# One-pass layer norm with the scale moved to the mask and to adj, and squares summed before the norm product, in a two-layer graph kernel

## The chip, the cores and the metric

The kernel runs on one core of a Trainium2 chip. The metric is the device time of one execution in microseconds (us). The runs of one kernel agreed within 0.12%; the mean granted TensorE clock of the timed runs was 0.996 to 0.999. TensorE is called PE in the profile (PEld is its weight load), VectorE is DVE, ScalarE is ACT, GpSimd is POOL. L128 is line 128 of the kernel; the numbers differ between kernels, so the tile names (pg, pv, pn ...) are the better guide. PSUM is the memory into which the matmuls of this kernel write, and a record is one instruction as the profile lists it.

## The reference, cut to what matters

x is (64, 256, 512) fp32, adj is (256, 256) of zeros and ones with 3% ones.

```python
# layer 0
h = jnp.maximum(_layernorm(x), 0.0)
q, k, v = h @ Wq.T, h @ Wk.T, h @ Wv.T          # per batch element, written as einsums
rel = adj.T[None] * (q @ k^T)
rel = rel / jnp.linalg.norm(rel, axis=2, keepdims=True)
x = x + rel @ v
# layer 1
h = jnp.maximum(_layernorm(x), 0.0)
x = x + (adj @ h) @ weight + bias
```

## The kernel before

It works on 32 pairs of batch elements (512 tokens in four chunks of 128). All matmuls are fp32. `pt` are TensorE transposes of h, `pg` and `pv` the two projections of layer 0, `prel` the scores, `pu` the product with v, `pn` the row norms, `py` and `po` the two products of layer 1. The parts that the change and the argument touch:

```python
def norm_relu(dst, src):                      # both layers; tiles st, mv, rs left out
    for c in range(TC):
        nc.vector.bn_stats(st[:, c, :], src[:, c, :])
        nc.vector.bn_aggr(mv[:, c, :], st[:, c, :])
    nc.vector.tensor_scalar(rs, mv[:, :, 1], 0.0, EPS, op0=ALU.max, op1=ALU.add)
    nc.scalar.activation(rs, rs, AF.Sqrt)
    nc.vector.reciprocal(rs, rs)
    for c in range(TC):
        nc.vector.tensor_scalar(dst[:, c, :], src[:, c, :], mv[:, c, 0:1], rs[:, c : c + 1],
                                op0=ALU.subtract, op1=ALU.mult)
        nc.vector.scalar_tensor_tensor(dst[:, c, :], dst[:, c, :], 0.0, dst[:, c, :],
                                       op0=ALU.is_gt, op1=ALU.mult)
# ... scores(i): prel matmuls, then for each batch element b
            nc.vector.tensor_mul(rel[:, b], pm, adj_sb)
            nc.scalar.activation(sq[:, b], rel[:, b], AF.Square)
# ... attend(i): pu matmuls, then the norm product
                for m in range(NC):
                    nc.tensor.matmul(pn[:, c : c + 1], sq[:, b, m, ts(n, P)], ones,
                                     start=(m == 0), stop=(m == NC - 1))
# ... ln1(i): norm_relu, then the bias is added to the residual on GpSimd
            nc.gpsimd.tensor_tensor(X[i][:, c, :], X[i][:, c, :], bias_bc, ALU.add)
# ... the loop over pairs
    for i in range(NP):
        # ... load(i + 3)
        scores(i)
        if nxt:
            transposes(i + 1)
        attend(i)
        ln1(i)
        if nxt:
            project_g(i + 1); project_v(i + 1)
        # ... ln0(i + 2)
        gather_mix(i)                         # py, po, output
```

Of the kernel before, what the change touches and what calls it, by code (L numbers as in the profile page):

```python
# [9 lines left out]
F32 = mybir.dt.float32  # L10
AF = mybir.ActivationFunctionType
ALU = mybir.AluOpType
EPS = 1e-5
# [3 lines left out]
def kernel(  # L17
# [8 lines left out]
    bias: bass.AP,  # L26
    out: bass.AP,
):
    """Two pre-norm graph layers, worked on two batch elements (512 tokens) at a time.

    Layer 0 uses q k^T = h (Wq^T Wk) h^T with Wq^T Wk formed once, keeps the masked
    scores transposed ([m, n], so that adj is read as it lies and the scores are the
    stationary operand of the product with v), and divides by the row norms after that
    product.  Layer 1 forms (adj h)^T directly, so it needs no transposes of h.
    The residual stream of a pair stays in one SBUF tile from its load to its store.
    """
    nc = tc.nc
    P = 128
    B, N, D = x.shape
    DC = D // P  # L40
    NC = N // P
    NB = 2
    TC = NB * NC
    T = NB * N
# [7 lines left out]
    work = ctx.enter_context(tc.tile_pool(name="work", bufs=2))  # L52
    small = ctx.enter_context(tc.tile_pool(name="small", bufs=3))
# [1 line left out]
    ps_m = ctx.enter_context(tc.tile_pool(name="ps_m", bufs=5, space=bass.MemoryType.PSUM))  # L55
    ps_n = ctx.enter_context(tc.tile_pool(name="ps_n", bufs=1, space=bass.MemoryType.PSUM))

    X, H, HT, G, V, R, H2 = {}, {}, {}, {}, {}, {}, {}

    def load(i):  # L60
        X[i] = xpool.tile([P, TC, D], F32, tag="x", name=f"x_{i}")
        nc.sync.dma_start(out=X[i], in_=xs[i])

# [1 line left out]
    load(0)  # L65
    ident = const.tile([P, P], F32, name="ident")
    make_identity(nc, ident)
    ones = const.tile([P, 1], F32, name="ones")
# [8 lines left out]
    adj_sb = const.tile([P, NC, N], F32, name="adj_sb")  # L77
# [5 lines left out]
        out=bias_bc, in_=bass.AP(tensor=bias.tensor, offset=bias.offset, ap=[[0, P], [1, D]])  # L83
    )

    def norm_relu(dst, src):
        """dst = max(layernorm(src), 0), as (t > 0) * t so that a NaN stays one.

        A row with a NaN has one as its mean; its variance is kept out of the square root.
        """  # L90
        st = small.tile([P, TC, 6], F32, tag="st", name="st")
        mv = small.tile([P, TC, 2], F32, tag="mv", name="mv")
        rs = small.tile([P, TC], F32, tag="rs", name="rs")
        for c in range(TC):
            nc.vector.bn_stats(st[:, c, :], src[:, c, :])  # L95
            nc.vector.bn_aggr(mv[:, c, :], st[:, c, :])
        nc.vector.tensor_scalar(rs, mv[:, :, 1], 0.0, EPS, op0=ALU.max, op1=ALU.add)
        nc.scalar.activation(rs, rs, AF.Sqrt)
        nc.vector.reciprocal(rs, rs)
        for c in range(TC):  # L100
            nc.vector.tensor_scalar(  # L101
                dst[:, c, :], src[:, c, :], mv[:, c, 0:1], rs[:, c : c + 1],
                op0=ALU.subtract, op1=ALU.mult,
            )
            nc.vector.scalar_tensor_tensor(  # L105
                dst[:, c, :], dst[:, c, :], 0.0, dst[:, c, :], op0=ALU.is_gt, op1=ALU.mult
            )

# [1 line left out]
    def ln0(i):  # L110
        H[i] = work.tile([P, TC, D], F32, tag="h", name=f"h_{i}")
        norm_relu(H[i], X[i])

    def transposes(i):
        h = H.pop(i)
# [27 lines left out]
            nc.scalar.copy(V[i][:, c, :], pm[:, :D])  # L143

    def scores(i):
        ht, g = HT.pop(i), G.pop(i)
        rel = work.tile([P, NB, NC, N], F32, tag="rel", name=f"rel_{i}")
        sq = work.tile([P, NB, NC, N], F32, tag="sq", name=f"sq_{i}")
        for b in range(NB):
            pm = ps_m.tile([P, NC, N], F32, tag="pm", name="prel")  # L150
            for m in range(NC):
                for e in range(DC):
                    nc.tensor.matmul(  # L153
                        pm[:, m, :], ht[:, e, ts(b * NC + m, P)], g[:, e, ts(b, N)],
                        start=(e == 0), stop=(e == DC - 1),
                    )
            nc.vector.tensor_mul(rel[:, b], pm, adj_sb)  # L157
            nc.scalar.activation(sq[:, b], rel[:, b], AF.Square)  # L158
        R[i] = (rel, sq)

    def attend(i):
        (rel, sq), v = R.pop(i), V.pop(i)
        pu = []
        for b in range(NB):
            for n in range(NC):
                pm = ps_m.tile([P, 512], F32, tag="pm", name="pu")
                for m in range(NC):
                    nc.tensor.matmul(  # L168
                        pm[:, :D], rel[:, b, m, ts(n, P)], v[:, b * NC + m, :],
                        start=(m == 0), stop=(m == NC - 1),  # L170
                    )
                pu.append(pm)
        pn = ps_n.tile([P, TC], F32, tag="pn", name="pn")
        for b in range(NB):
            for n in range(NC):
                c = b * NC + n
                for m in range(NC):
                    nc.tensor.matmul(  # L178
                        pn[:, c : c + 1], sq[:, b, m, ts(n, P)], ones,
                        start=(m == 0), stop=(m == NC - 1),  # L180
                    )
        rn = small.tile([P, TC], F32, tag="rn", name="rn")
        nc.scalar.activation(rn, pn, AF.Sqrt)  # L183
        nc.vector.reciprocal(rn, rn)  # L184
        for c in range(TC):
            nc.vector.scalar_tensor_tensor(  # L186
                X[i][:, c, :], pu[c][:, :D], rn[:, c : c + 1], X[i][:, c, :],
                op0=ALU.mult, op1=ALU.add,
            )

# [1 line left out]
    def ln1(i):  # L192
        H2[i] = work.tile([P, TC, D], F32, tag="h2", name=f"h2_{i}")
        norm_relu(H2[i], X[i])
        for c in range(TC):
            nc.gpsimd.tensor_tensor(X[i][:, c, :], X[i][:, c, :], bias_bc, ALU.add)  # L196

    def gather_mix(i):
        h2, xt = H2.pop(i), X.pop(i)
        yt = work.tile([P, DC, T], F32, tag="yt", name=f"yt_{i}")  # L200
        for b in range(NB):
            for d0 in range(0, DC, 2):
                pm = ps_m.tile([P, 2, N], F32, tag="pm", name="py")
                for d in range(2):
                    for m in range(NC):
                        nc.tensor.matmul(  # L206
                            pm[:, d, :], h2[:, b * NC + m, ts(d0 + d, P)], adjt_sb[:, m, :],
                            start=(m == 0), stop=(m == NC - 1),
                        )
                nc.scalar.copy(yt[:, d0 : d0 + 2, ts(b, N)], pm)  # L210
        for c in range(TC):
            pm = ps_m.tile([P, 512], F32, tag="pm", name="po")
            for d in range(DC):
                nc.tensor.matmul(  # L214
                    pm[:, :D], yt[:, d, ts(c, P)], w_sb[:, d, :],
                    start=(d == 0), stop=(d == DC - 1),
                )
            nc.vector.tensor_add(xt[:, c, :], pm[:, :D], xt[:, c, :])  # L218
        nc.gpsimd.dma_start(out=outs[i], in_=xt)  # L219

# [1 line left out]
    m_sb = const.tile([P, DC, D], F32, name="m_sb")  # L222
    for d in range(DC):
        pm = ps_m.tile([P, 512], F32, tag="pm", name="pw")
        for e in range(DC):
            nc.tensor.matmul(  # L226
                pm[:, :D], wq_sb[:, e, ts(d, P)], wk_sb[:, e, :],
                start=(e == 0), stop=(e == DC - 1),
# [8 lines left out]
    adjt_sb = const.tile([P, NC, N], F32, name="adjt_sb")  # L237
# [3 lines left out]
            nc.tensor.transpose(pt[:, m * N + n * P : m * N + (n + 1) * P], adj_sb[:, n, ts(m, P)], ident)  # L241
    nc.scalar.copy(adjt_sb, pt[:, : NC * N].rearrange("p (m n) -> p m n", m=NC))

# [1 line left out]
    ln0(0)  # L245
    for j in (1, 2):
        if j < NP:
# [4 lines left out]
    if NP > 1:  # L252
        ln0(1)
    for i in range(NP):
        nxt = i + 1 < NP
        if i + 3 < NP:
            load(i + 3)
# [6 lines that stand above are left out]
            project_g(i + 1)  # L264
            project_v(i + 1)
        if i + 2 < NP:
            ln0(i + 2)
        gather_mix(i)
# [28 lines left out]
```

## Time and profile before

| | before |
|---|---|
| median time | 2161.83 us (2160.5 to 2161.97, 3 runs) |
| TensorE busy | 98% of the span |
| VectorE, ScalarE, GpSimd busy | 38%, 16%, 12% |
| period of one pair on TensorE | 65.64 us |
| TensorE's waits at the start, in the last pair | 19.7 us, 9.9 us |

A period is read from the chain in order of time: the distance between the starts of the same group, here pv, in two pairs that follow each other. It repeats within 0.02 us in all middle pairs of a trace.

### The profile page before, as it was taken

To read this page: it belongs to the slowest core of one execution; us is meant where nothing else is said; L and a number is where in the kernel's file an instruction comes from. 1 tells how busy PE (TensorE), PEld (TensorE's weight loads), DVE (VectorE), ACT (ScalarE), POOL (GpSimd) and SP (SyncE) were. 2 spreads that over 40 slices of the span, in tenths; PEclk is the share of its full clock that TensorE was granted. 3 is DMA by queue.
4 is the path that set the end of the run, shared out by engine and by line. 5 is a ranking of instruction groups with operands and counts; after the bars stand their busy time and mean duration, and the time that the engine had idled before them with its cause. 6 is when DMAs were issued, how large, how long until landed. Compare 5 with 4: busy or idle time off the path is not lost.

```text
span 2159.8 us, 16275 instructions
## 1 busy us (share of the span) xinstructions
PE 2122.4 (98%) x6708; PEld 1190.1 (55%) x6708; DVE 812.5 (38%) x1504; ACT 348.9 (16%) x682; POOL 257.0 (12%) x170
## 2 busy tenths in 40 slices
PE   6999999999999999999999999999999999999996
PEld 3555555555555555555555555555555555555554
DVE  2422444323444324444234443234442244442333
ACT  1111111111111111111111111111111111111110
POOL 0101111101111001111011111011110011110111
PEclk9999999999999999999999999999999999999998
DMA  4011001111011110011110011110111100110001
GB/s 165 0 39 39 12 28 39 39 40 39 1 39 39 39 39 21 19 39 39 39 39 5 35 39 39 39 39 1 39 39 39 39 20 20 39 39 20 20 1 39
DMA packets 27689, 72.86 MB, mean 34 GB/s; under 512 B 1120, under 2 KB 1120, under 8 KB 27616
## 3 DMA queue, kind: packets, MB, share of 16 engines
q1 hardware_dynamic: 16896, 33.56, 4.6%
q0 software_dynamic: 9136, 35.13, 4.3%
q10 hardware_dynamic: 1584, 3.15, 0.4%
q8 instruction: 52, 0.85, 0.2%
q14 instruction: 21, 0.17, 0.0%
HBM read 38.27 MB, written 33.55 MB: 33 GB/s over the span
## 4 chain that ended last, share of the span: by engine, by line
PE 97%; issue 1%; DMA 1%; DVE 1%; POOL 0%; ACT 0%; POOLq 0%; ACTq 0%; DVEq 0%
PE pg L128 21%; PE pv L139 20%; PE po L214 20%; PE prel L153 10%; PE pu L168 10%; PE py L206 10%; PE pt L120 3%; PE pn L178 2%; DMA wk_sb<-in_L_gnn_Wk_dram 1%; PE pw L226 1%; POOL x L196 0%; DVE h L105 0%; DVE x L186 0%; DVE st L95 0%; DVE h L101 0%
## 5 line engine op out<-in xcount | busy, mean ns | idle before, releaser
L128 PE MATMUL pg<-ht,m_sb 128*128 128x512 f32 x1024 | 447.4, 595 | 0.0
L139 PE MATMUL pv<-wvt_sb,ht 128*128 128x512 f32 x1024 | 444.7, 592 | 0.0
L214 PE MATMUL po<-w_sb,yt 128*128 128x512 f32 x1024 | 444.7, 592 | 0.0
L218 DVE TENSOR_TENSOR x<-po,x 128x512 f32<-128x512 f32 x128 | 88.6, 692 | 777.7 <-PE po L214 777.7
L196 POOL TENSOR_TENSOR x<-x,bias_bc 128x512 f32<-128x512 f32 x128 | 229.5, 1821 | 850.3 <-DVE h L101 850.3
L139 PEld LDWEIGHTS pv<-wvt_sb,ht 128*128 128x128 f32 x1024 | 194.6, 190 | 244.9 <-issue 244.9
L214 PEld LDWEIGHTS po<-w_sb,yt 128*128 128x128 f32 x1024 | 194.6, 190 | 231.3 <-issue 229.6
L128 PEld LDWEIGHTS pg<-ht,m_sb 128*128 128x128 f32 x1024 | 192.0, 190 | 229.1 <-issue 228.2
L206 PE MATMUL py<-adjt_sb,h 128*128 128x256 f32 x1024 | 229.0, 382 | 9.9 <-DVE h L105 9.9
L105 DVE SCALAR_TENSOR_TENSOR h<-h 128x512 f32<-128x512 f32 x256 | 233.3, 953 | 0.0
L168 PE MATMUL pu<-v,rel 128*128 128x512 f32 x512 | 230.1, 592 | 0.0
L153 PE MATMUL prel<-g,ht 128*128 128x256 f32 x1024 | 226.2, 379 | 0.0
L206 PEld LDWEIGHTS py<-adjt_sb,h 128*128 128x128 f32 x1024 | 196.0, 192 | 50.7 <-issue 24.4
L153 PEld LDWEIGHTS prel<-g,ht 128*128 128x128 f32 x1024 | 194.6, 190 | 40.1 <-issue 15.3
L101 DVE TENSOR_SCALAR h<-x,mv,rs 128x512 f32<-128x512 f32 x256 | 186.7, 771 | 1.2
L95 DVE BATCH_NORM_STATS2 st<-x 128x6 f32<-128x512 f32 x256 | 167.3, 669 | 15.4 <-DMA x<-in_x_dram 15.4
L219 POOL DMA_DIRECT2D out_dram<-x x32 | 24.6, 770 | 1046.3 <-DVE x L218 1046.3
L168 PEld LDWEIGHTS pu<-v,rel 128*128 128x128 f32 x512 | 92.4, 190 | 92.4 <-issue 92.3
L158 ACT ACTIVATE sq<-rel 128x512 f32<-128x512 f32 x64 | 40.4, 631 | 545.3 <-DVE rel L157 545.3
L184 DVE RECIPROCAL rn<-rn 128x4 f32<-128x4 f32 x32 | 5.7, 178 | 319.0 <-ACT rn L183 319.0
L157 DVE TENSOR_TENSOR rel<-prel,adj_sb 128x512 f32<-128x512 f32 x64 | 44.3, 692 | 214.0 <-PE prel L153 214.0
L132 ACT COPY g<-pg 128x512 f32<-128x512 f32 x128 | 74.4, 581 | 289.0 <-PE pg L128 289.0
(33 smaller groups left out, 680.7 us busy)
## 6 DMA issues: line engine op xcount, KB each, us to landing
x<-in_x_dram SPq DMA_DIRECT2D x32, 1024.0 KB, 5.2
out_dram<-x POOLq DMA_DIRECT2D x32, 1024.0 KB, 4.7
wq_sb<-in_L_gnn_Wq_dram ACTq DMA_DIRECT2D x1, 1024.0 KB, 12.1
wk_sb<-in_L_gnn_Wk_dram ACTq DMA_DIRECT2D x1, 1024.0 KB, 18.4
wv_sb<-in_L_gnn_Wv_dram ACTq DMA_DIRECT2D x1, 1024.0 KB, 23.2
w_sb<-in_L_gnn_weight_dram POOLq DMA_DIRECT2D x1, 1024.0 KB, 11.7
adj_sb<-in_adj_dram POOLq DMA_DIRECT2D x1, 256.0 KB, 7.4
bias_bc<-in_L_gnn_bias_dram POOLq DMA_DIRECT2D x1, 256.0 KB, 12.4
```

Source lines behind the costliest of these rows:

```text
L95: nc.vector.bn_stats(st[:, c, :], src[:, c, :])
L101: nc.vector.tensor_scalar(dst[:, c, :], src[:, c, :], mv[:, c, 0:1], rs[:, c : c + 1], op0=ALU.subtract, op1=ALU.mult,)
L105: nc.vector.scalar_tensor_tensor(dst[:, c, :], dst[:, c, :], 0.0, dst[:, c, :], op0=ALU.is_gt, op1=ALU.mult)
L128: nc.tensor.matmul(pm[:, :T], m_sb[:, d, ts(e, P)], HT[i][:, d, :], start=(d == 0), stop=(d == DC - 1),)
L132: nc.scalar.copy(G[i][:, e, :], pm[:, :T])
L139: nc.tensor.matmul(pm[:, :D], HT[i][:, d, ts(c, P)], wvt_sb[:, d, :], start=(d == 0), stop=(d == DC - 1),)
L153: nc.tensor.matmul(pm[:, m, :], ht[:, e, ts(b * NC + m, P)], g[:, e, ts(b, N)], start=(e == 0), stop=(e == DC - 1),)
L168: nc.tensor.matmul(pm[:, :D], rel[:, b, m, ts(n, P)], v[:, b * NC + m, :], start=(m == 0), stop=(m == NC - 1),)
L196: nc.gpsimd.tensor_tensor(X[i][:, c, :], X[i][:, c, :], bias_bc, ALU.add)
L206: nc.tensor.matmul(pm[:, d, :], h2[:, b * NC + m, ts(d0 + d, P)], adjt_sb[:, m, :], start=(m == 0), stop=(m == NC - 1),)
L214: nc.tensor.matmul(pm[:, :D], yt[:, d, ts(c, P)], w_sb[:, d, :], start=(d == 0), stop=(d == DC - 1),)
L218: nc.vector.tensor_add(xt[:, c, :], pm[:, :D], xt[:, c, :])
```

## The change

The intent is to take work off VectorE and TensorE. A row's relu(layernorm) is relu(x - mean) times 1/std. That factor goes along with the token, so in layer 0 it is put into the mask (1/variance, since the token's factor enters its score and its v) and in layer 1 into a scaled copy of the transposed adj for each batch element. One pass of 128x512 takes the place of two. The squares of the two token chunks are summed on VectorE, so that the norm product needs 4 matmuls a pair in place of 8.

```diff
-        for c in range(TC):
-            nc.vector.tensor_scalar(dst, src, mean, rs, op0=ALU.subtract, op1=ALU.mult)
-            nc.vector.scalar_tensor_tensor(dst, dst, 0.0, dst, op0=ALU.is_gt, op1=ALU.mult)
+        for c in range(TC):     # arguments shortened here
+            nc.vector.tensor_scalar(dst, src, mean, 0.0, op0=ALU.subtract, op1=ALU.max)
 ... layer 0: r2 = 1/var (+ 0 * mean, to keep a NaN), std = sqrt(var)
-            nc.vector.tensor_mul(rel[:, b], pm, adj_sb)
-            nc.scalar.activation(sq[:, b], rel[:, b], AF.Square)
+            for m in range(NC):
+                c = b * NC + m
+                nc.vector.scalar_tensor_tensor(
+                    rel[:, b, m, :], pm[:, m, :], r2[:, c : c + 1], adj_sb[:, m, :],
+                    op0=ALU.mult, op1=ALU.mult,
+                )
+                nc.scalar.activation(
+                    sq[:, b, m, :], rel[:, b, m, :], AF.Square, scale=std[:, c : c + 1]
+                )
+        nc.vector.tensor_add(sqs, sq[:, :, 0, :], sq[:, :, 1, :])
 ...
-                for m in range(NC):
-                    nc.tensor.matmul(
-                        pn[:, c : c + 1], sq[:, b, m, ts(n, P)], ones,
-                        start=(m == 0), stop=(m == NC - 1),
-                    )
+                nc.tensor.matmul(
+                    pn[:, c : c + 1], sqs[:, b, ts(n, P)], ones, start=True, stop=True
+                )
 ... layer 1: rs = 1/sqrt(var) (+ 0 * mean)
+                nc.scalar.activation(
+                    adjb[:, b, m, :], adjt_sb[:, m, :], AF.Copy, scale=rs[:, c : c + 1]
+                )
 ...
-                            pm[:, d, :], h2[:, b * NC + m, ts(d0 + d, P)], adjt_sb[:, m, :],
+                            pm[:, d, :], h2[:, b * NC + m, ts(d0 + d, P)], adjb[:, b, m, :],
```

More of the change, by code (lines that the diff above doesn't have):

```diff
@@ L56 @@
     ps_n = ctx.enter_context(tc.tile_pool(name="ps_n", bufs=1, space=bass.MemoryType.PSUM))
-    X, H, HT, G, V, R, H2 = {}, {}, {}, {}, {}, {}, {}
+    X, H, HT, G, V, R, H2, SC = {}, {}, {}, {}, {}, {}, {}, {}
     def load(i):
@@ L84, with stats @@
     )
-    def norm_relu(dst, src):
+    def stats(src):
         st = small.tile([P, TC, 6], F32, tag="st", name="st")
         mv = small.tile([P, TC, 2], F32, tag="mv", name="mv")
-        rs = small.tile([P, TC], F32, tag="rs", name="rs")
+        ve = small.tile([P, TC], F32, tag="ve", name="ve")
         for c in range(TC):
@@ L96, in norm_relu, with keep_nan, centred_relu @@
             nc.vector.bn_aggr(mv[:, c, :], st[:, c, :])
-        nc.vector.tensor_scalar(rs, mv[:, :, 1], 0.0, EPS, op0=ALU.max, op1=ALU.add)
-        nc.scalar.activation(rs, rs, AF.Sqrt)
-        nc.vector.reciprocal(rs, rs)
+        nc.vector.tensor_scalar(ve, mv[:, :, 1], 0.0, EPS, op0=ALU.max, op1=ALU.add)
+        return mv, ve
+    def keep_nan(dst, mv, src):
+        nc.vector.scalar_tensor_tensor(dst, mv[:, :, 0], 0.0, src, op0=ALU.mult, op1=ALU.add)
+    def centred_relu(dst, src, mv):
         for c in range(TC):
             nc.vector.tensor_scalar(
-                dst[:, c, :], src[:, c, :], mv[:, c, 0:1], rs[:, c : c + 1],
-                op0=ALU.subtract, op1=ALU.mult,
-            )
-            nc.vector.scalar_tensor_tensor(
-                dst[:, c, :], dst[:, c, :], 0.0, dst[:, c, :], op0=ALU.is_gt, op1=ALU.mult
+                dst[:, c, :], src[:, c, :], mv[:, c, 0:1], 0.0, op0=ALU.subtract, op1=ALU.max
             )
@@ L111, in ln0 @@
         H[i] = work.tile([P, TC, D], F32, tag="h", name=f"h_{i}")
-        norm_relu(H[i], X[i])
+        mv, ve = stats(X[i])
+        r2 = small.tile([P, TC], F32, tag="r2", name="r2")
+        std = small.tile([P, TC], F32, tag="std", name="std")
+        nc.vector.reciprocal(r2, ve)
+        keep_nan(r2, mv, r2)
+        nc.scalar.activation(std, ve, AF.Sqrt)
+        centred_relu(H[i], X[i], mv)
+        SC[i] = (r2, std)
     def transposes(i):
@@ L145, in scores @@
     def scores(i):
-        ht, g = HT.pop(i), G.pop(i)
+        ht, g, (r2, std) = HT.pop(i), G.pop(i), SC.pop(i)
         rel = work.tile([P, NB, NC, N], F32, tag="rel", name=f"rel_{i}")
@@ L156, in scores @@
                     )
-            nc.vector.tensor_mul(rel[:, b], pm, adj_sb)
-            nc.scalar.activation(sq[:, b], rel[:, b], AF.Square)
-        R[i] = (rel, sq)
+            for m in range(NC):
[7 more added lines that the diff above has]
+                )
+        sqs = work.tile([P, NB, N], F32, tag="sqs", name=f"sqs_{i}")
+        nc.vector.tensor_add(sqs, sq[:, :, 0, :], sq[:, :, 1, :])
+        R[i] = (rel, sqs)
     def attend(i):
-        (rel, sq), v = R.pop(i), V.pop(i)
+        (rel, sqs), v = R.pop(i), V.pop(i)
         pu = []
@@ L176, in attend @@
                 c = b * NC + n
-                for m in range(NC):
-                    nc.tensor.matmul(
-                        pn[:, c : c + 1], sq[:, b, m, ts(n, P)], ones,
-                        start=(m == 0), stop=(m == NC - 1),
-                    )
+                nc.tensor.matmul(
+                    pn[:, c : c + 1], sqs[:, b, ts(n, P)], ones, start=True, stop=True
+                )
         rn = small.tile([P, TC], F32, tag="rn", name="rn")
@@ L192, in ln1 @@
     def ln1(i):
-        H2[i] = work.tile([P, TC, D], F32, tag="h2", name=f"h2_{i}")
-        norm_relu(H2[i], X[i])
+        h2 = work.tile([P, TC, D], F32, tag="h2", name=f"h2_{i}")
+        adjb = work.tile([P, NB, NC, N], F32, tag="adjb", name=f"adjb_{i}")
+        mv, ve = stats(X[i])
+        rs = small.tile([P, TC], F32, tag="rs", name="rs")
+        nc.scalar.activation(rs, ve, AF.Sqrt)
+        nc.vector.reciprocal(rs, rs)
+        keep_nan(rs, mv, rs)
+        centred_relu(h2, X[i], mv)
+        for b in range(NB):
+            for m in range(NC):
+                c = b * NC + m
+                nc.scalar.activation(
+                    adjb[:, b, m, :], adjt_sb[:, m, :], AF.Copy, scale=rs[:, c : c + 1]
+                )
+        H2[i] = (h2, adjb)
         for c in range(TC):
@@ L198, in gather_mix @@
     def gather_mix(i):
-        h2, xt = H2.pop(i), X.pop(i)
+        (h2, adjb), xt = H2.pop(i), X.pop(i)
         yt = work.tile([P, DC, T], F32, tag="yt", name=f"yt_{i}")
```

## The prediction

> **What bounds the kernel now.** I read the page's first part, then the chain of waits that ended last, then the costliest groups of TensorE, and last the timeline of one pair of batch elements. The page:
>
> ```profile
> PE 2122.4 (98%) x6708; PEld 1190.1 (55%) x6708; DVE 812.5 (38%) x1504; ACT 348.9 (16%) x682; POOL 257.0 (12%) x170
> ...
> PE 97%; issue 1%; DMA 1%; DVE 1%; POOL 0%; ACT 0%; POOLq 0%; ACTq 0%; DVEq 0%
> PE pg L128 21%; PE pv L139 20%; PE po L214 20%; PE prel L153 10%; PE pu L168 10%; PE py L206 10%; PE pt L120 3%; PE pn L178 2%; DMA wk_sb<-in_L_gnn_Wk_dram 1%; PE pw L226 1%; POOL x L196 0%; DVE h L105 0%; DVE x L186 0%; DVE st L95 0%; DVE h L101 0%
> ```
>
> TensorE is busy 98% of the span, and the chain stays on it for 97%. VectorE's 812.5 us and ScalarE's 348.9 us run beside it. So only two things can shorten the kernel: fewer or shorter matmuls, or less of the little time in which TensorE waits. The waits of TensorE itself are:
>
> ```profile
> PE pw L226 <- DMA wk_sb<-in_L_gnn_Wk_dram: 19.7, 1, 19.7
> PE py L206 <- DVE h L105: 9.9, 2, 9.5
> ```
>
> The first is the load of the weights at the start, which the change leaves alone. The second comes once, in the last pair, where no next pair covers the layer norm of layer 1. All other pairs repeat every 65.64 us: the chain has the pv group start at 1019.25 and again at 1084.89.
>
> The matmul that the change halves, in the groups by shape and in a timeline window of one pair:
>
> ```profile
> L178 PE MATMUL pn<-ones,sq 128*128 128x1 f32 x512 | 58.9, 245 | 0.0
> ```
> ```profile
> 1003.57 1.84 PE L178 MATMUL pn<-ones,sq 128*128 128x1 f32 x16
> ...
> 1005.27 13.98 PE L128 MATMUL pg<-ht,m_sb 128*128 128x512 f32 x32
> ```
>
> The reader is to see that a pair has 16 records (the program has 8, each fp32 matmul leaves two) and that they hold TensorE from 1003.57 to 1005.27, 1.70 us, or 0.106 us a record; the mean of 245 ns is latency, since records overlap.
>
> A second, small loss is in the order of transposes and products, in the same pair one step on:
>
> ```profile
> 1061.24 1.02 PE L168 MATMUL pu<-v,rel 128*128 128x512 f32 x2
> 1061.54 0.63 ACT L158 ACTIVATE sq<-rel 128x512 f32<-128x512 f32 x1
> ...
> 1062.07 1.91 ACT L121 COPY ht<-pt 128x512 f32<-128x512 f32 x3
> 1062.10 1.26 PE L120 MATMUL pt<-ident,h 128*128 128x128 f32 x8
> ...
> 1062.70 0.42 PEld L120 LDWEIGHTS pt<-ident,h 128*128 128x128 f32 x4 [0.24 <-ACT ht L121]
> 1063.09 0.30 PEld L168 LDWEIGHTS pu<-v,rel 128*128 128x128 f32 x2
> 1063.19 1.02 PE L168 MATMUL pu<-v,rel 128*128 128x512 f32 x2
> ```
>
> The last eight transposes hold TensorE for 1.09 us (1062.10 to 1063.19), the first eight 0.87 us (1060.37 to 1061.24). The fourth group of four needs a PSUM buffer that ScalarE's second copy frees; the copy stood behind the square, and TensorE lost 0.22 us.
>
> **What the Trainium skill says.** TensorE: Matmul & The Clock Gate, LDWEIGHTS: a weight load takes about P/1.2 ns, P its columns, so 107 ns for 128. The trace agrees: 106 ns a record, though only one column is streamed. The norm product is bound by its weight loads, so halving their number halves its time. FP8 and Floating Point Precision, TensorE Precision Notes: true fp32 takes four passes. With the 2.4 GHz gap of N/2.4 + 2.5 ns (first page, Back-to-back issue gap) that makes an estimate of 4 x 216 = 863 ns for 512 columns; the trace has 13.73 us for 16 of pv, 858 ns. The big products run at their floor and cannot gain. SBUF — State Buffer, Who interferes with whom: VectorE with two SBUF inputs, or in a two-port mode, blocks against GpSimd. The trace agrees: in the last pair, beside the bias add, two passes of L105 took 3.42 us where two took 1.29 us elsewhere.
>
> **The change part by part.**
> 1. Norm product: 4 program matmuls a pair in place of 8, so 8 records x 0.106 us = 0.85 us, x 32 pairs = **27.2 us**, all of it on the path. The sum of squares that allows it, one 128x512 add on VectorE, is about 0.69 us (the like add L218), 22 us in all, hidden: squares are done near 1062.4, so the sum near 1063.2, and pn starts at 1069.2.
> 2. Layer norm, second pass removed on VectorE (L105, 233.3 us). The first pass stays in form, 517 to 544 ns where nothing interferes. Off the path except in the last pair.
> 3. Mask: two 128x512 multiplies (692 ns) become four 128x256 with a pointer scalar. From L186 (745 ns for 512 elements, of which 512/0.96 = 533 ns stream) I estimate 212 + 267 = 479 ns, 61 us in all for 44. The second half is ready near 1060.57 + 0.96 = 1061.53, where the products that need it begin after 1064: no wait.
> 4. ScalarE: 128 squares of 256 for 64 of 512, and 128 scaled copies of adj^T. Estimated from the square's 631 ns: 631 - 213 (256/1.2) = 418, near 450 ns with a pointer for scale; +18 and +58 us, total some 425 us of 2130. The copies end some 10 us after pn; py starts 27.5 us after it. Hidden.
> 5. Order. The instruction order of the changed kernel has the transposes as 8, pu, 4, pu, 4 instead of 8, pu, 8. A pu lasts 0.86 us, so the fourth group is wanted near 1063.4, and the second copy, behind two short squares, ends near 1063.0. The 0.22 us should go: 31 x 0.22 = 6.8 us at most; I count **5 us**.
> 6. Last pair: from the end of pn (2119.3) to po (2138.82) is 19.5 us, 6.91 of them py's work. New chain after pn: root and reciprocal 0.5, residual 2.73, statistics to the variance 2.77 with two centred passes between them 1.0, then root, reciprocal, two more passes and the NaN step 1.5 to 3.5 (GpSimd's bias add interferes), a scaled copy 0.4: 8.9 to 10.9, plus py 6.9 without stalls. That gains 1.7 to 3.7; I count **2 us**.
>
> The large products keep shape and number. Sum: 2161.8 - 27.2 - 5 - 2 = 2127.6, so 2128 us, 1.6% less.
>
> **Rivals.**
> (a) VectorE's 200 us of saved passes come through. Against it: TensorE waits for VectorE only 9.9 us in all. For a 2% gain the saving must reach 43 us; parts 1, 5 and 6 at their largest give 27.2 + 6.8 + 3.7 = 37.7, so about 2124.
> (b) A new wait replaces the loads: the chain mask, square, sum, pn now crosses to ScalarE and back to VectorE. It has some 6 us of slack by the times in part 1; only a ScalarE blocked behind its in-order queue could use it up. If each pair lost 0.85 us there, the time would stay at 2155.
> (c) ScalarE's root or scaled copies hold back the copies of g, and so PSUM. The copies of g are 3.4 us apart and take 0.6; four scaled copies take some 1.8 us. If each pair lost 0.3 us, 2138.
> (d) The order gain of part 5 does not come, the rest does: 2133.
>
> **Range and chances.** The norm term is almost certain, which puts everything without new waits between 2124 and 2135; half a chance of a small loss as in (c) widens it to 2121 to 2140. Faster by 2% would need 2118.6, below what the terms give: 3%. Slower by 2%: 1%, for a wait that I have not seen. Within 2%: 96%.
>
> **What would show it right or wrong.** pn with 256 records and about 27 us on the chain; a period of about 64.6 us between pairs; VectorE near 620 us and ScalarE near 425; no wait of TensorE for squares, sums or scaled copies except the last pair's; the fourth group of transposes without a wait for ScalarE. A period above 65 us with TensorE idle ahead of pn, pu or pg would make the prediction wrong.

## The result, and the profile after

The changed kernel took 2127.65 us (median of 4 runs, 2127.24 to 2128.48), the kernel before 2161.59 in the same rounds. The ratio is 0.9846, with a 95% interval of 0.9832 to 0.986. A ratio here is taken from the runs of both kernels, and is not quite the ratio of the medians. The result lies within 0.4 us of the predicted 2128 and is 1.5% faster, in the class "within 2%".

The page of the changed kernel, the engines and the chain:

```profile
PE 2086.4 (98%) x6452; PEld 1160.6 (55%) x6452; DVE 642.0 (30%) x1408; ACT 417.3 (20%) x874; POOL 209.2 (10%) x170
...
PE 97%; issue 1%; DMA 1%; DVE 0%; POOL 0%; ACT 0%; POOLq 0%; ACTq 0%; DVEq 0%
PE pg L136 21%; PE pv L147 21%; PE po L247 20%; PE prel L165 10%; PE pu L189 10%; PE py L239 10%; PE pt L128 3%; PE pn L198 1%; DMA wk_sb<-in_L_gnn_Wk_dram 1%; PE pw L259 1%; POOL x L229 0%; DVE x L205 0%; DVE st L94 0%; ACT wvt_sb L269 0%; POOLq L325 0%
```

VectorE gave up 170 us of busy time and ScalarE took on 68, and TensorE is still at 98% and still is the chain. Its busy time fell by 36 us, its records by 256, all of them pn. The waits of TensorE and the group of pn:

```profile
PE pw L259 <- DMA wk_sb<-in_L_gnn_Wk_dram: 19.7, 1, 19.7
...
PE py L239 <- ACT adjb L224: 11.3, 1, 11.3
```
```profile
L198 PE MATMUL pn<-ones,sqs 128*128 128x1 f32 x256 | 30.3, 240 | 0.0
```

The wait at the start is as before. The wait in the last pair did not shrink: it grew from 9.9 to 11.3 us and is now for the scaled copies of adj. One pair in the timeline (first column the start, second the duration):

```profile
1044.26 1.02 PE L189 MATMUL pu<-v,rel 128*128 128x512 f32 x2
...
1045.12 0.60 PE L128 MATMUL pt<-ident,h 128*128 128x128 f32 x4
...
1045.56 1.02 PE L189 MATMUL pu<-v,rel 128*128 128x512 f32 x2
1045.99 0.14 PEld L128 LDWEIGHTS pt<-ident,h 128*128 128x128 f32 x1 [0.24 <-ACT ht L129]
1046.42 0.60 PE L128 MATMUL pt<-ident,h 128*128 128x128 f32 x4
...
1046.85 5.32 PE L189 MATMUL pu<-v,rel 128*128 128x512 f32 x12
...
1052.01 0.95 PE L198 MATMUL pn<-ones,sqs 128*128 128x1 f32 x8
...
1052.82 13.98 PE L136 MATMUL pg<-ht,m_sb 128*128 128x512 f32 x32
```

Two things are to be seen. pn holds TensorE from 1052.01 to 1052.82, 0.81 us where it had held it for 1.70. And a product of 0.86 us now lies between the two last groups of transposes: the weight load still waits for ScalarE's copy (0.24 us), but it does so while that product runs, and the two groups take 0.44 and 0.43 us in place of 1.09 together.

The period is 64.53 us (pv starts at 1002.27 and 1066.79), 1.11 less. The spans of the two profiled runs differ by 2159.8 - 2125.1 = 34.7 us. The first pv starts 0.35 us earlier (55.35 and 55.00), which is within scatter: over the kernels here that load in the same way it starts between 54.34 and 55.56 us; from there to the last pv it is 2014.13 and 1979.70 us, 34.43 less; from the last pv to the end it is 90.32 and 90.40, so the last pair gained nothing although its pn is 0.89 us shorter. That sets the question: two terms in the pairs, and a loss of about 1 us at the end.

### The profile page after: what moved, and what is told of

Same layout as the page of the kernel before. It is cut to its first block, busy times and chain, and to the rows that moved or that the text cites. A ratio compares the mean times of both kernels' runs of the same rounds, so it can differ in the third digit from the quotient of the medians.

```text
span 2125.1 us, 15806 instructions
## 1 busy us (share of the span) xinstructions
PE 2086.4 (98%) x6452; PEld 1160.6 (55%) x6452; DVE 642.0 (30%) x1408; ACT 417.3 (20%) x874; POOL 209.2 (10%) x170
## 4 chain that ended last, share of the span: by engine, by line
PE 97%; issue 1%; DMA 1%; DVE 0%; POOL 0%; ACT 0%; POOLq 0%; ACTq 0%; DVEq 0%
PE pg L136 21%; PE pv L147 21%; PE po L247 20%; PE prel L165 10%; PE pu L189 10%; PE py L239 10%; PE pt L128 3%; PE pn L198 1%; DMA wk_sb<-in_L_gnn_Wk_dram 1%; PE pw L259 1%; POOL x L229 0%; DVE x L205 0%; DVE st L94 0%; ACT wvt_sb L269 0%; POOLq L325 0%
## 5 line engine op out<-in xcount | busy, mean ns | idle before, releaser
L229 POOL TENSOR_TENSOR x<-x,bias_bc 128x512 f32<-128x512 f32 x128 | 181.6, 1448 | 727.9 <-DVE mv L95 727.9
L239 PE MATMUL py<-adjb,h 128*128 128x256 f32 x1024 | 228.5, 382 | 11.3 <-ACT adjb L224 11.3
L189 PE MATMUL pu<-v,rel 128*128 128x512 f32 x512 | 235.3, 593 | 0.0
L239 PEld LDWEIGHTS py<-adjb,h 128*128 128x128 f32 x1024 | 196.0, 192 | 51.7 <-issue 14.8
L175 ACT ACTIVATE sq<-rel,std 128x256 f32<-128x256 f32 x128 | 58.1, 502 | 538.5 <-DVE rel L171 538.5
L105 DVE TENSOR_SCALAR h<-x,mv 128x512 f32<-128x512 f32 x256 | 147.2, 576 | 0.0
L151 ACT COPY v<-pv 128x512 f32<-128x512 f32 x128 | 75.0, 586 | 347.4 <-PE pv L147 347.4
L171 DVE SCALAR_TENSOR_TENSOR rel<-prel,r,adj_sb 128x256 f32<-128x256 f32 x128 | 56.1, 479 | 215.3 <-PE prel L165 215.3
L243 ACT COPY yt<-py 128x512 f32<-128x512 f32 x128 | 75.0, 586 | 147.9 <-PE py L239 147.9
```

The source lines that it names most:

```text
L151: nc.scalar.copy(V[i][:, c, :], pm[:, :D])
L189: nc.tensor.matmul(pm[:, :D], rel[:, b, m, ts(n, P)], v[:, b * NC + m, :], start=(m == 0), stop=(m == NC - 1),)
L239: nc.tensor.matmul(pm[:, d, :], h2[:, b * NC + m, ts(d0 + d, P)], adjb[:, b, m, :], start=(m == 0), stop=(m == NC - 1),)
L243: nc.scalar.copy(yt[:, d0 : d0 + 2, ts(b, N)], pm)
```

## The experiments

My theory is three terms: the norm product, 32 x 0.89 = 28.5 us; the order of transposes and products, 31 x 0.22 = 6.8 us; the last pair, minus 1 us. The main rival is that the relief of VectorE, whose normalising passes were cut by half, carries part of the gain. The medians of the kernel before that stand beside these runs are 2161.34 us (for e1, e2, e3 and e4) and 2161.42 us (for e3c, e5, e6 and e9). All eight kernels gave correct results.

### e1_norm_only: the norm product alone

```diff
 (kernel before)
-        R[i] = (rel, sq)
+        sqs = work.tile([P, NB, N], F32, tag="sqs", name=f"sqs_{i}")
+        nc.vector.tensor_add(sqs, sq[:, :, 0, :], sq[:, :, 1, :])
+        R[i] = (rel, sqs)
 ... pn: 4 matmuls on sqs instead of 8 on sq, as in the change
```

> The kernel before with one part of the change alone: the squares of the two token chunks are summed on VectorE and the norm product takes 4 matmuls a pair. Layer norm, mask and the order of transposes and products stay as before. Theory (three terms: norm product 28.5 us, order of the transposes 6.8 us, last pair minus 1): 2161.6 - 28.5 = 2133 us, period between pairs 64.75 us. Rival (the time comes from the passes taken off VectorE): no more than a third of the 34 us, 2150 or above.

Measured: 2132.26 us (ratio 0.9865), period 64.74. VectorE's busy time is 836.6 us here, more than the 812.5 of the kernel before, and still 29 us are gone. The period fell by 0.90 us. The rival is out as the main cause.

### e2_norm_undone: the change without the norm product

```diff
 (changed kernel)
-        sqs = ...; nc.vector.tensor_add(sqs, ...)
-        R[i] = (rel, sqs)
+        R[i] = (rel, sq)
 ... pn: 8 matmuls on sq, as before
```

> The changed kernel with that part undone: 8 norm matmuls a pair on the squares themselves, no sum on VectorE; one-pass layer norm, scaled mask and new order kept. Theory: 2127.6 + 28.5 = 2156 us, period 65.4 us. Rival (VectorE's relief carries the gain): at or below 2140.

Measured: 2155.48 us (ratio 0.9974), period 65.42. All the relief of VectorE is in this kernel (619.8 us busy), and the new order too, and together they are worth 0.3%, the size of the order term alone (next section). With e1 this is the same term from the other side: 65.42 - 64.53 = 0.89 us a pair.

### e3_order_only and e3c_halves_control: where the 0.22 us come from

Both split the mask and the squares of the kernel before into halves. In the first the halves take a scalar per partition (ones), and the order of TensorE's instructions then comes out as in the changed kernel; in the control they take none, and the order stays.

```diff
 (kernel before; e3_order_only)
-            nc.vector.tensor_mul(rel[:, b], pm, adj_sb)
-            nc.scalar.activation(sq[:, b], rel[:, b], AF.Square)
+            for m in range(NC):
+                nc.vector.scalar_tensor_tensor(rel[:, b, m, :], pm[:, m, :], one4[:, m : m + 1],
+                    adj_sb[:, m, :], op0=ALU.mult, op1=ALU.mult)
+                nc.scalar.activation(sq[:, b, m, :], rel[:, b, m, :], AF.Square, scale=one4[:, m : m + 1])
 (e3c_halves_control: 1.0 in place of one4[...], and no scale)
```

> The kernel before with its mask and squares in halves of 256 columns that take a scalar per partition (ones, so the values stay). This adds work to VectorE and ScalarE and removes none, but the order of instructions on TensorE becomes that of the changed kernel (transposes 8, product, 4, product, 4). Theory: the 0.22 us a pair go, 2161.6 - 6.8 = 2154.8 us, period 65.42 us. Rival (the order is of no account, more work beside TensorE costs a little): 2161 to 2164.

> Control for the order experiment: the kernel before with its mask and squares in halves of 256 columns, but without a scalar per partition; the order on TensorE stays as before (transposes 8, product, 8, product). Theory (the order, not the size of the pieces, takes the wait away): no gain, 2160 to 2163 us, period near 65.64. Rival (it is the shorter pieces on ScalarE that let the copy come in time): about 2155.

Measured: 2154.77 us (ratio 0.9969) and period 65.42 for the first, 2163.86 us (ratio 1.0015) and period 65.73 for the control. So the order is worth 65.64 - 65.42 = 0.22 us a pair, though the kernel that has it does more work on VectorE (824.1 us) and ScalarE (363.4) than the kernel before. With e1 the two terms add up: 0.90 + 0.22 = 1.12 us a pair, against 1.11 for the whole change. The new order in the timeline of e3_order_only, a product before and after the last group of transposes:

```profile
1059.67 0.59 PE L173 MATMUL pu<-v,rel 128*128 128x512 f32 x1
1060.10 0.60 PE L122 MATMUL pt<-ident,h 128*128 128x128 f32 x4
...
1060.53 5.32 PE L173 MATMUL pu<-v,rel 128*128 128x512 f32 x12
```

Why the toolchain orders TensorE's instructions otherwise when the halves take a scalar per partition was not looked into. Shorter pieces alone cost 0.09 us a pair. The timeline of the control shows why:

```profile
1062.44 1.35 PE L120 MATMUL pt<-ident,h 128*128 128x128 f32 x8
...
1063.13 0.42 PEld L120 LDWEIGHTS pt<-ident,h 128*128 128x128 f32 x4 [0.33 <-ACT ht L121]
...
1063.63 4.89 PE L171 MATMUL pu<-v,rel 128*128 128x512 f32 x11
```

The two last groups of transposes take 1.19 us (1062.44 to 1063.63), against 1.09 in the kernel before: two short squares hold ScalarE longer than one long one (0.72 us against 0.63), its copy comes later (the weight load waits 0.33 us for it, not 0.24), and nothing lies between the groups to cover that.

### e4_second_pass: VectorE's relief taken back

```diff
 (changed kernel, in centred_relu, after the one pass)
+            nc.vector.scalar_tensor_tensor(
+                dst[:, c, :], dst[:, c, :], 0.0, dst[:, c, :], op0=ALU.is_gt, op1=ALU.mult
+            )
```

> The changed kernel with the second pass of the layer norm put back on VectorE (256 passes of 128x512; the rectified values are unchanged by it). Theory: the pairs hide it all, period stays 64.53 us, and only the last pair's open chain grows by 3 to 5 us: 2131 to 2133 us. Rival (VectorE's relief carries part of the gain): the period grows and the time goes to 2140 or more.

Measured: 2126.98 us (2125.73 to 2127.37), period 64.53. The page's engine line:

```profile
PE 2086.4 (98%) x6452; PEld 1160.7 (55%) x6452; DVE 832.3 (39%) x1664; ACT 413.8 (19%) x874; POOL 230.9 (11%) x170
```

VectorE works 190 us more and the kernel is not slower at all: the relief is worth nothing in any pair, since the period is the same. The expected 3 to 5 us in the last pair did not come either. There the instruction order put the passes of the last two chunks behind the short instruction that the scaled copies wait for, and that one fell between two of GpSimd's adds and took 0.15 us instead of 1.22. The wait in the last pair was 10.7 us, not 11.3. I had summed the passes as if all of them stood in front.

### e5_last_bias_dve: what the last pair waits for

```diff
 (changed kernel, ln1)
-            nc.gpsimd.tensor_tensor(X[i][:, c, :], X[i][:, c, :], bias_bc, ALU.add)
+            eng = nc.gpsimd if i + 1 < NP else nc.vector
+            eng.tensor_tensor(X[i][:, c, :], X[i][:, c, :], bias_bc, ALU.add)
```

> The changed kernel with the bias add of the last pair alone moved from GpSimd to VectorE, behind its layer norm. Theory (in the last pair three VectorE instructions of 1.2 to 1.4 us are short ones that waited for GpSimd's bias add): they take 0.15 to 0.5 us, the open chain shortens by 3 us, 2124.6 us. Rival (these instructions are long for themselves): 2127.6, unchanged.

The timeline of the last pair, first of the changed kernel:

```profile
2089.93 5.65 POOL L229 TENSOR_TENSOR x<-x,bias_bc 128x512 f32<-128x512 f32 x4 [18.97 <-DVE mv L95]
2090.22 1.23 DVE L96 TENSOR_SCALAR ve<-mv 128x4 f32<-128x4 f32 x1
...
2091.84 1.39 DVE L105 TENSOR_SCALAR h<-x,mv 128x512 f32<-128x512 f32 x1
2093.16 1.22 DVE L101 SCALAR_TENSOR_TENSOR rs<-mv,rs 128x4 f32<-128x4 f32 x1
2094.41 1.70 ACT L224 ACTIVATE adjb<-adjt_sb,rs 128x256 f32<-128x256 f32 x4 [2.72 <-DVE rs L101]
2094.97 9.36 PE L239 MATMUL py<-adjb,h 128*128 128x256 f32 x32 [11.33 <-ACT adjb L224]
```

and then of this experiment:

```profile
2090.78 0.16 DVE L96 TENSOR_SCALAR ve<-mv 128x4 f32<-128x4 f32 x1
...
2091.33 0.46 DVE L105 TENSOR_SCALAR h<-x,mv 128x512 f32<-128x512 f32 x1
2091.70 0.16 DVE L101 SCALAR_TENSOR_TENSOR rs<-mv,rs 128x4 f32<-128x4 f32 x1
```

Measured: 2123.59 us (2122.88 to 2124.76). An instruction on 4 columns takes 1.23 us beside GpSimd's add of 512 columns and 0.16 us without it; the three together take 3.84 and 0.78 us. The three are the two short ones and one pass of 512 columns (L105). The wait of TensorE fell by 3.0 us (11.3 to 8.3), as expected. The medians differ by 4.1 us and the spans of the profiled runs by 2.4, of which the first pv, 0.56 us later here, hides some; the trace is the better measure of so small a term. The changed kernel had put onto the path of the last pair three instructions that the add holds up; in the kernel before it was the second pass of the norm that was held up. The new norm also lets the add start sooner: its pass over x needs only the mean, so in the changed kernel the first pass is over and the add begins at 2089.93, just before the variance plus epsilon (2090.22). In the kernel before the like instruction (L97, 0.17 us) ran at 2125.32 and the add began at 2126.61. The same happens in every pair: L101 of layer 1 took 1.22 us in all 32, but only in the last does TensorE wait for it.

### e6_tail_filled and e9_start_and_tail: the edges

In the tail the trace shows a second loss. The granted clock of TensorE in stretches of 2 us of the changed kernel (columns: stretch, length, busy us and instructions of PE, PEld, DVE, ACT, POOL, then the granted clock, DMA share and GB/s):

```profile
2086.00:2088.00 2.00, 0.00 (x0) 0.00 (x0) 2.00 (x5) 0.00 (x0) 0.00 (x0) 0.50 0.00 0
...
2096.00:2098.00 2.00, 2.00 (x6) 1.64 (x5) 0.00 (x0) 0.11 (x1) 0.00 (x0) 0.50 0.00 0
...
2100.00:2102.00 2.00, 2.00 (x11) 1.75 (x10) 0.00 (x0) 0.59 (x1) 0.00 (x0) 1.00 0.00 0
```

The changed kernel's clock is at half from about 2085.8, some 2 us after the last pn, and full again at about 2099.4, some 4.5 us after work is back (both worked out from the mean of the stretch in which it changes, 0.95 and 0.64). So py takes 9.2 us (2094.97 to 2104.17) in place of 6.91. The kernel before shows the same 0.50, from 1.3 us after its last pn, and e5 too, from 2.8 us after (worked out in the same way, from stretches of 0.64 and 0.74). The experiment lets the last layer 1 products of the pair before cover the wait; the second one adds the loads at the start in the order of need; there adj stays on GpSimd's queue and the bias moves to ScalarE's.

```diff
 (changed kernel, the loop over pairs; e6 and e9)
-        gather_mix(i)
+        if i == NP - 1 and NP > 1:
+            gather_mix(i - 1)
+        if i != NP - 2:
+            gather_mix(i)
 (e9 only: one queue, in this order, then x of pairs 1 and 2, then the layer 1 weight)
+    nc.sync.dma_start(out=wq_sb, in_=wq.rearrange("(c p) d -> p c d", p=P))
+    nc.sync.dma_start(out=wk_sb, in_=wk.rearrange("(c p) d -> p c d", p=P))
+    load(0)
+    nc.sync.dma_start(out=wv_sb, in_=wv.rearrange("(c p) d -> p c d", p=P))
```

> The changed kernel with the last two pairs' ends interleaved: the products of layer 1 of the last pair but one are issued after the attention of the last pair, so that they cover its layer norm. Theory: the 11.3 us in which TensorE waits and the some 2.3 us by which its slowed clock stretches the products after the wait both go, 2127.6 - 13.6 = 2114 us. Rival (the clock is low there for another reason than the wait): 2116 to 2117, and the py of the last pair still takes over 9 us.

> The one before it with the loads at the start put in one queue in the order of need: Wq, Wk, x of the first pair, Wv, then x of the next two pairs and the layer 1 weight. Theory: Wq and Wk are 2 MB and land near 8.5 us (an estimate from 390 GB/s in the first 20 us and 2 us to begin), not at 19.7, so TensorE begins 11 us earlier: about 2103 us. Rival (one queue is slower, or the layer norm of the first pair or Wv becomes the wait): 2108 to 2114.

The line of TensorE for the last pair's py in e6_tail_filled, without a wait and with a start of the next group 6.9 us later, and the stretch of that py with its granted clock of 1.00:

```profile
2084.09 7.07 PE L239 MATMUL py<-adjb,h 128*128 128x256 f32 x32
...
2090.99 13.90 PE L247 MATMUL po<-w_sb,yt 128*128 128x512 f32 x32
```
```profile
2084.00:2091.00 7.00, 7.00 (x34) 6.08 (x33) 0.69 (x1) 1.75 (x3) 0.77 (x1) 1.00 0.40 150
```

Measured: 2112.89 us (ratio 0.9777) for e6 and 2105.82 us (2105.7 to 2106.69; ratio 0.9746, interval 0.9732 to 0.9759) for e9, which beats both kernels. The tail is worth 14.8 us between the medians, where 13.6 were expected: the wait of 11.3 us and the slow clock's 2.3 are both gone, and the granted clock is 1.00 through the last py. The spans of the two profiled runs differ by 13.1 us, with a first pv 0.50 us later in e6, so that the traces give the 13.6; the rest of the 14.8 is not placed. The start gave 7.1 us and not 11: both theories missed, by 3 us and by 2. The wait is in the trace:

```profile
PE pw L258 <- DMA wk_sb<-in_L_gnn_Wk_dram: 12.5, 1, 12.5
```

The trace has the DMA engines move 151, 248 and 359 GB/s in the three stretches of 2 us from 2 to 8 us, and about 390 only from then on; in the changed kernel, whose loads are spread over three queues, it was 179, 387 and 394. So a slower start of the loads, as the rival had it, is part of it; that the single queue is what makes it slow is not shown, since the order of the loads differs too. Nor is it all: Wq and Wk did not have the engines to themselves, since adj and the bias came by other queues and x of the first pair was queued right behind them. The shares are left open; Wq and Wk on two queues were not tried.

## Why the prediction was right, point by point

| step | predicted | measured | by |
|---|---|---|---|
| 1 norm product | 27.2 us | 0.89 to 0.90 us a pair, x 32 = 28.5 to 28.8 | e1, e2 |
| 2 VectorE's second pass | 0 in the pairs | 0 in the pairs, and no gain at the end | e4 |
| 3 mask in halves | no wait | none; 479 ns each, as estimated | trace |
| 4 ScalarE's added work | no wait, about 425 us | no wait in the pairs, 417.3 us; squares 502 and copies 497 ns (450 estimated) | trace |
| 5 order | 5 us (6.8 at most) | 0.22 us a pair, x 31 = 6.8 | e3, e3c |
| 6 last pair | gain of 2 us | loss of 1.0 us | trace, e5 |
| start | 0 | 0.35 us, within scatter | trace |

The measured terms add up to 28.5 + 6.8 - 1.0 + 0.35 = 34.65 us, against 34.7 between the spans. The prediction had 34.2. It was right in its mechanism and in the two large terms, and it hit the total a little by luck: the norm product and the order gave 3 us more than counted, and step 6 gave 3 us less.

**Step 6 is the step that failed.** It counted 17.5 us from the end of pn to po (19.5 less 2), and 20.5 were measured. The prediction has "root, reciprocal, two more passes and the NaN step 1.5 to 3.5 (GpSimd's bias add interferes)" behind statistics and two passes of 2.77 + 1.0. The trace shows the interference one instruction earlier too: the variance plus epsilon on 4 columns took 1.23 us. From the end of pn to the first py it was 11.3 us, above the whole range of 8.9 to 10.9 and 0.7 above the 10.6 that a gain of 2 needs. The larger part is the other one: "plus py 6.9 without stalls" was wrong, since py took 9.2 us, 2.3 more, as its first 4.5 us ran at half clock. The kernel before showed that as well: its py took 9.6 us beside a wait of 0.4, of which the prediction counted only 6.91 as work. Looking at the clock column of that stretch before predicting would have told.

**Step 1 was 5% short.** 16 records took 1.70 us and 8 took 0.81; the prediction had divided 1.70 by two. The eight records that went had taken 0.89 us, 0.111 us each, so the time of a block is not quite in proportion to its number of records; why is not shown.

**Steps 3 and 4** estimated the halves from a time per column that the trace of the kernel before does not show. The runs now do: on VectorE 745 ns for 512 columns and 479 for 256; on ScalarE 631 for 512, 411 for 256 without a scale operand (e3c), and 502 with one, which is where the 450 was short.

**The rivals.** Rival (a), VectorE's relief, is refuted by e4, which adds 190 us to VectorE and no time. The waits (b) and (c) did not appear: the period of the changed kernel is shorter by just the two terms. In (b)'s chain the sum of squares ended at 1046.13 in the pair shown, and pn began at 1052.01, 5.9 us of slack where 6 had been read. Rival (d), no gain by order, is refuted by e3. The VectorE figure was the only one clearly off among the signs named: 642.0 us, not 620. The two short instructions of layer 1 that GpSimd's add held in each pair, up to 1243 and 1225 ns, added some 68 us (L96 44.6 us in place of 10.5; L101 of layer 1 39.0 against 4.8 in layer 0); the pass that was to stay in form took 147.2 us in place of 186.7 and hid over half of that.

## What to carry to other kernels

When one engine is the chain for 97%, count only what leaves that engine, and compare the instruction order on it before and after: here a reordering nobody had asked for was worth a fifth of the gain, while 170 us less work on VectorE were worth nothing. A matmul record whose moving operand is one column still cost about 0.11 us here, the time of its weight load, so where another engine has time, sum the stationary operands there first. Then look at the first and the last stage, where nothing overlaps: filling the last wait with the work of the pair before gave 13.6 us by the traces (14.8 by the medians), of which 2.3 were the half clock that TensorE had come to in its wait and kept for 4.5 us of the work that followed.

## What the Trainium skill lacked or had wrong

- TensorE: Matmul & The Clock Gate, LDWEIGHTS: P/1.2 ns holds for one-column products (101 to 111 ns a record, from 0.81 us for 8 and from the 0.89 us that 8 more took, against 107), but I found no page that says that each fp32 matmul of the program stands in the profile as two records, each with its own load (16 records for 8 matmuls; 429 ns of TensorE for one record of 512 columns). The count of loads, and so the gain, depends on it.
- The same page, What's actually happening (two states of the clock, half after an idle window of some 3.4 us): the two states agree, the time does not. The clock halved 1.3, 2.2 and 2.8 us after the last pn (kernel before, changed kernel, e5), less than an idle window (3.0 us in the changed kernel if the 0.81 us of pn is counted as idle, which no run here decides). In the changed kernel it came back some 4.5 us after work did, and stretched a 6.91 us group to 9.2 us. The page counts the ramp as below 1% of a kernel; here it was 2.3 us of 2127, 0.1%, so that it agrees; with the wait before it, it was 13.6 us, the largest loss left at the end.
- SBUF — State Buffer, Who interferes with whom: the lock for the whole instruction agrees. It has no number for tiny instructions: those of 4 columns took 1.22 to 1.24 us beside a GpSimd add and 0.15 us without.
- DMA: Bandwidth & Descriptors: I found no rates there for the first microseconds of a kernel. With most loads on one queue (e9) the engines moved 151, 248 and 359 GB/s in three successive stretches of 2 us before they reached 390; with the loads spread over three queues 179, 387 and 394. The cause was not tested.
